# A graph layer on one core: 8 of 17 quads of edges grouped instead of 4 of 9, and their work moved in the order

## The chip, the cores and the metric

The kernel runs on one core of one Trainium2 chip. The metric is the time of one execution on the device in microseconds (us); less is better. A core has TensorE (PE, matrix products, with its weight loads listed apart as PEld), VectorE (DVE), ScalarE (ACT), GpSimd (POOL) and SyncE (SP, which here only issues transfers). TensorE writes to PSUM, which the kernel cuts into eight tiles of 512 f32 columns a partition (tags A and B, four each).

## The reference

One layer of a graph network on 6250 nodes with 128 features and 200000 edges; a node's messages are summed over its edges.

```python
h = jnp.maximum(_layernorm(x, axis=-1), 0.0)
...
idx_i = pair_indices[0]      # src: random in 0..6249
idx_j = pair_indices[1]      # dst: sorted
x = atomic_embedding @ W_in
W_ij = shifted_softplus(f_ij @ W_f1 + b_f1) @ W_f2 + b_f2
W_ij = W_ij * f_ij_cutoff
x_ij = x[idx_j] * W_ij
out = jax.ops.segment_sum(x_ij, idx_i, num_segments=N_ATOMS)
return shifted_softplus(out @ W_o1 + b_o1) @ W_o2 + b_o2
```

The result is added to the layer's input. An edge has 20 features and one cutoff weight. Edges are sorted by dst, from which they read, and not by src, to which their messages are added.

## The kernel before

**Tiling.** 128 edges are a chunk, four chunks a quad; 1563 chunks make 391 quads, and the main loop (L1220 on) takes one a step, in software-pipelined stages: at step i TensorE multiplies the edge features of quad i + 1 (`s1_pe`, z, L326) and, for quad i - 1, reads its 128-row inputs from a window of the node table by a one-hot product (xg, L510) and makes the filter (W, L507 and L518); ScalarE takes exp and ln of z and scales xg by the cutoff (xc, L523); VectorE multiplies W by xc (`s2_m`, L533), which gives the 512 messages of the quad. Node features are prepared along the way in 25 groups (`prep_*`), edge features split into three bf16 parts in 49 blocks (`fb_*`, L276 to L299).

**Three ways for a message.** The list `mpq` names the quads that are *grouped*; before, four of every nine from quad 8 on, 168 in all. The other 223 go by GpSimd.

- *Plain* quads (31: the first 12 and the last 19 of those not grouped): VectorE compares all pairs of src in a chunk (`s1_eq`, eq, L370), TensorE adds up messages of the same src (pp, L545), ScalarE copies, and GpSimd adds each chunk to one of four accumulators in DRAM by an indirect transfer (`scatter`, L595). Edges that aren't the first of their src go to a row that nobody reads.
- *Listed* quads (192, in 12 windows of 16): duplicates are found ahead of time, in pairs of quads (`l_eq`, L382, `l_count`, L391); messages are scattered straight from the tile s, and a window's duplicates go to rows of their own, which are summed and scattered later (`l_*`).
- *Grouped* quads use no scatter for most edges. Nodes are cut into 16 groups of 392. For eight quads at a time VectorE ranks edges within their group (`rank_*`, L601 to L669) and gives each of them one of 32 slots of its group or one of 64 overflow slots. `perm_oh` (L675) makes the one-hot of slots, `part_rem` (L689) splits the messages (tile pt, two buffers) into high and remaining bf16 parts, `permute` (pq, L700) puts them in slots by sixteen products of 387 columns, and `perm_out` (L706) copies each of four slices. After eight quads, a *round*, four *unit* calls (`unit_oh` L779, `unit_pe` un, L794, `unit_evac` L805) add the slots to the nodes of four groups each, in SBUF (accT), by 96 products on 32 rows each. Steps with a unit call are those of `unit_its`; `clear` moves other TensorE work out of their way.
- *Overflow* of a grouped quad (64 slots): `over_pe` (po, L715 to L717) gathers it by twelve products on 64 columns, in the lower or upper half of a tile that two grouped quads share; these also add up the three parts; `over_out` (L723) copies the sum into mo. For each such pair duplicates are summed by a product (`over_row`, `over_eq`, `over_sum`) and 128 rows are scattered.

**Order.** It is written out by hand: `at(step, point, function)` files work under a step and a point of it, and the loop runs the points in a fixed order; each engine takes its own instructions in that order. What matters here: "L" (loads, SP's queue), then on VectorE "D0", oh, "D1", eq, "DM", the message product, index work, "D2"; on TensorE xg and W of i - 1, z of i + 1, pp of i - 2, then "PE2"; on ScalarE the activations, "A0", "A1", xc, then what "PE2" and "A2" bring. Within a point, hooks run in the order in which they were filed. A buffer that is taken again waits for its last reader, wherever that stands in the order of another engine.

**Start and end.** Before the loop the accumulators' zeros begin to be written (GpSimd's and SP's queues, until about step 23). `RET` retires the first accumulator for the last 64 scatters, and it is added to accT by 13 transposes (`r0_*`) while the loop ends. After the last scatter the other three are loaded, summed, transposed and added (tp, L1388), and two products with the activation between them and the layer's input make the result.

## Time and profile before

Three runs took 2062.51, 2064.37 and 2069.87 us, median 2064.37. The profiled execution took 2051.26 us.

| | us | share of the span |
|---|---|---|
| profiled execution, whole | 2051.26 | |
| its span, first to last instruction | 2049.5 | 100% |
| TensorE busy | 1855.4 | 91% |
| VectorE busy | 1658.4 | 81% |
| GpSimd busy | 1636.9 | 80% |
| ScalarE busy | 1491.2 | 73% |
| mean granted clock of TensorE | | 0.966 of full speed |

In the profile's rows a group stands as line, engine, operation, tile written <- tiles read, shape and count, then busy time and mean duration of one, then the idle time of the engine just before them and what ended it. Matmuls overlap, so their busy time is less than count times duration. Rows of waits read: engine and line, what it waited for, us in total, times, longest. Timelines give start, duration and count.

### The profile page before, as it was taken

To read this page: it belongs to the slowest core of one execution; us is meant where nothing else is said; L and a number is where in the kernel's file an instruction comes from. 1 tells how busy PE (TensorE), PEld (TensorE's weight loads), DVE (VectorE), ACT (ScalarE), POOL (GpSimd) and SP (SyncE) were. 2 spreads that over 40 slices of the span, in tenths; PEclk is the share of its full clock that TensorE was granted. 3 is DMA by queue.
4 is the path that set the end of the run, shared out by engine and by line. 5 is a ranking of instruction groups with operands and counts; after the bars stand their busy time and mean duration, and the time that the engine had idled before them with its cause. 6 is when DMAs were issued, how large, how long until landed. Compare 5 with 4: busy or idle time off the path is not lost. (4 is left out here: it accounts for less than half of the span.)

```text
span 2049.5 us, 57496 instructions
## 1 busy us (share of the span) xinstructions
PE 1855.4 (91%) x20381; PEld 1284.7 (63%) x20381; DVE 1658.4 (81%) x4449; ACT 1491.2 (73%) x4083; POOL 1636.9 (80%) x1040
## 2 busy tenths in 40 slices
PE   3579999999999999999999999999999999999966
PEld 2456666666666666666666666666666666677734
DVE  4578898798888888988888978879898887787745
ACT  3468776877777788777778777777877778788714
POOL 3578888888888888887878778888888888888884
PEclk9689999999999999999999999999999999999987
DMA  6887666667666676766667666676676666666747
GB/s 239 228 210 154 124 123 121 129 110 140 126 126 119 118 139 119 131 127 120 120 121 132 120 117 123 110 125 127 121 131 108 129 126 109 112 123 125 141 44 252
DMA packets 359686, 272.58 MB, mean 133 GB/s; under 512 B 97727, under 2 KB 319850, under 8 KB 359394
## 3 DMA queue, kind: packets, MB, share of 16 engines
q0 software_dynamic: 143728, 71.30, 34.9%
q1 hardware_dynamic: 215378, 197.50, 32.9%
q8 instruction: 161, 2.64, 0.5%
q14 instruction: 131, 1.07, 0.2%
q10 hardware_dynamic: 288, 0.07, 0.0%
HBM read 154.45 MB, written 114.24 MB: 131 GB/s over the span
## 5 line engine op out<-in xcount | busy, mean ns | idle before, releaser
L595 POOL DMA_INDIRECT acc<-s,lji x768 | 1242.7, 1618 | 254.5 <-issue 185.8
L700 PE MATMUL pq<-pt,pm 128*128 128x387 bf16 x2688 | 533.6, 342 | 33.6 <-DVE pt L689 10.5
L523 ACT ACTIVATE xc<-xg,cb 128x128 f32<-128x128 f32 x1564 | 447.7, 372 | 111.5 <-PE xg L510 101.8
L518 PE MATMUL W<-w,a 128*128 128x128 f32 x3128 | 465.3, 293 | 0.0
L518 PEld LDWEIGHTS W<-w,a 128*128 128x128 f32 x3128 | 389.6, 196 | 42.3 <-issue 3.1
L706 ACT CAST mst<-pq 128x387 bf16<-128x387 f32 x672 | 303.7, 482 | 135.0 <-PE pq L700 132.3
L700 PEld LDWEIGHTS <-pm 128*128 128x128 bf16 x2688 | 261.0, 99 | 221.5 <-issue 26.6
L794 PE MATMUL un<-so,mst 32*128 32x392 bf16 x8064 | 371.0, 326 | 12.9 <-DVE pr L640 6.4
L794 PEld LDWEIGHTS <-mst 32*128 32x128 bf16 x8064 | 223.9, 93 | 153.4 <-issue 51.0
L336 ACT ACTIVATE a<-a,con 128x512 f32<-128x512 f32 x391 | 282.3, 722 | 12.8
L331 ACT ACTIVATE a<-z 128x512 f32<-128x512 f32 x391 | 237.8, 608 | 32.9 <-PE z L326 18.0
L595 POOL DMA_INDIRECT acc<-s,ji x123 | 196.0, 1594 | 78.7 <-issue 26.5
L689 DVE TENSOR_TENSOR pt<-pt 128x512 f32<-128x512 f32 x336 | 231.7, 689 | 5.8
L675 DVE TENSOR_SCALAR pm<-iot,pos 128x576 bf16<-128x576 f16 x672 | 221.0, 390 | 0.0
L533 DVE TENSOR_TENSOR s<-W,xc 128x512 f32<-128x512 f32 x192 | 131.9, 687 | 89.1 <-ACT xc L523 84.9
L805 DVE TENSOR_TENSOR accT<-un,accT 128x392 f32<-128x392 f32 x320 | 158.5, 558 | 55.1 <-PE un L794 55.0
L779 DVE TENSOR_SCALAR so<-iot,mst 128x392 bf16<-128x392 f16 x672 | 192.6, 346 | 5.4 <-PE un L794 5.3
L595 POOL DMA_INDIRECT acc<-os,oji x96 | 156.9, 1635 | 30.7 <-issue 15.6
L510 PE MATMUL xg<-wn,oh 63*128 63x128 bf16 x1564 | 157.5, 222 | 14.8 <-ACT xc L523 8.2
L326 PE MATMUL z<-ft,ws 123*128 123x512 bf16 x391 | 151.9, 389 | 15.7 <-POOL b2rep L940 9.3
L507 PE MATMUL W<-b2rep,onesb 64*128 64x512 bf16 x391 | 154.1, 394 | 0.0
L533 DVE TENSOR_TENSOR pt<-W,xc 128x512 f32<-128x512 f32 x168 | 115.3, 686 | 44.1 <-ACT xc L523 36.0
(210 smaller groups left out, 2431.3 us busy)
## 6 DMA issues: line engine op xcount, KB each, us to landing
rb<-reld SPq DMA_DIRECT2D x391, 64.0 KB
fsd<-f SPq DMA_DIRECT2D x49, 480.0 KB
ft<-fsd SPq DMA_DIRECT2D x195, 120.0 KB
sb<-src SPq DMA_DIRECT2D x169, 128.0 KB
fb<-in_fB_dram SPq DMA_DIRECT2D x49, 320.0 KB
ft<-fsd SPq DMA_DIRECT2D x195, 80.0 KB
wn<-tab SPq DMA_DIRECT2D x782, 15.8 KB
acc<-s,lji POOLq DMA_INDIRECT x768
```

The lines of the kernel that those rows point to most:

```text
L331: nc.scalar.activation(a, st[q]["z"], AF.Exp)
L336: nc.scalar.activation(a, a, AF.Ln, bias=half, scale=0.5)
L518: nc.tensor.matmul(W[:, c, :], st[q]["a"][:, c * P:(c + 1) * P], w2, start=False, stop=(c == 3))
L523: nc.scalar.mul(xc[:, c, :], st[q]["xg"][:, c, :], late["c", q // CQ][:, 4 * (q % CQ) + c:4 * (q % CQ) + c + 1])
L533: nc.vector.tensor_tensor(m[:, :, :P], st[q]["W"], st[q]["xc"], op=ALU.mult)
L595: nc.gpsimd.indirect_dma_start(out=accs[k][:rows, :], out_offset=bass.IndirectOffsetOnAxis(ap=ji, axis=0), in_=s, in_offset=None, compute_ ...
L675: nc.vector.tensor_scalar(pm[:, c], iot[:, :SLOTS], rk[r]["pos"][:, 4 * j + c:4 * j + c + 1], None, op0=ALU.is_equal)
L689: nc.vector.tensor_tensor(pt[:, :, k * P:(k + 1) * P], a, high(a), op=ALU.subtract)
L700: nc.tensor.matmul(t[:, :PW], mp[q]["pm"][:, c, s * P:(s + 1) * P], high(mp[q]["pt"][:, c:c + 1, :PW])[:, 0], start=(c == 0), stop=(c == 3))
L706: nc.scalar.copy(mp[q]["ms", s][:, :PW], mp[q].pop(("q", s))[:, :PW])
L779: nc.vector.tensor_scalar(so, iotw[:, :GN], w[:, 3 * P // 2:3 * P // 2 + 1], None, op0=ALU.is_equal)
L794: nc.tensor.matmul(ts[g][:, :GN], mp[q]["ms", s][v, k * P:(k + 1) * P], mp[q]["oh"][v], start=(q == qs[0] and k == 0), stop=(q == qs[-1] a ...
```

## The change

The list of grouped quads starts at 2 and takes 8 of 17, which makes 184 of 391; 176 quads are listed, in 11 windows, and 31 are plain. A round still has eight quads and four unit calls, now at four evenly spaced steps of the 17. Two new points are run right before pp: "DR", where `part_rem` now stands, and "PE1", where `over_pe` and `over_out` now stand, for both quads of a pair at once, in the step in which the next pair's first message is multiplied. `over_pe` issues four products for each quad, alternately for the lower and the upper 64 columns, on all three parts at 387 columns; mo holds the parts in bf16, and `over_sum` makes three bf16 products in place of one f32. Rank steps lie at fixed distances before their first quad. Splits of edge features (`fb_*`) and loads and comparisons of listed quads are moved to unit steps, and the maximum of a block (`fb_max`) to three steps earlier. The two halves of the second index load lie in unused columns of accT. The fourth accumulator's zeros are issued by step 20. The scratch for GpSimd's descriptors is set to 8192 bytes, where it stood at the default.

```diff
@@ -25,13 +25,13 @@
...
 SLOTS = GRP * CAP + OVC
-MP0 = 8
-MPGAPS = (2, 2, 2, 3)
+MP0 = 2
+MPGAPS = (2, 2, 2, 2, 2, 2, 2, 3)
 MPEND = 0
...
 RKQ = 8
-UOFF = (2, 6)
+UOFF = (2, 6, 10, 14)
 SW = 16
...
@@ -77,7 +77,7 @@
...
     K1_END, K2_END, K3_END = 2, 8, 140
-    Z2, Z3 = [0,0,1,1,2,2,3,3,4,4], [5+2*j for j in range(10)]
+    Z2, Z3 = [0,0,1,1,2,2,3,3,4,4], [5, 7, 9, 11, 13, 14, 16, 17, 19, 20]
     mpq = sorted_quads(NQ)
...
@@ -150,7 +150,7 @@
...
     for i in range(2):
-        mo_ = cp.tile([P, 132], F32, name=f"mo{i}")
+        mo_ = cp.tile([P, PW + 1], BF16, name=f"mo{i}")
         mos.append(mo_)
...
@@ -169,8 +169,8 @@
...
         v = accs[k][ACC_R:].rearrange("(p t) f -> p (t f)", p=P)
-        w = LR // ZL
-        nc.sync.dma_start(v[:, j * w:(j + 1) * w], zero[:, :w])
+        a, b = j * LR // ZL, (j + 1) * LR // ZL
+        nc.sync.dma_start(v[:, a:b], zero[:, :b - a])
 
...
@@ -283,8 +283,10 @@
...
 
+    def fb_max(b):
+        nc.vector.tensor_reduce(fmax[:, b:b + 1], fst[b]["f"], axis=AX.X, op=ALU.max, apply_absolute_value=True)
+
     def fb_2(b):
-        nc.vector.tensor_reduce(fmax[:, b:b + 1], fst[b]["f"], axis=AX.X, op=ALU.max, apply_absolute_value=True)
         fr = wk.tile([P, FE], F32, tag="fr", name="fr", bufs=1)
...
@@ -706,29 +708,25 @@
...
     def over_pe(q):
-        h = mpi[q] % 2 * OVC
+        qs = mpq[mpi[q] // 2 * 2:mpi[q] + 1]
         t = ps.tile([P, 512], F32, tag="B", name="po", bufs=4)
-        o = t[h:h + OVC]
         for c in range(4):
-            w = mp[q]["pm"][:, c, GRP * CAP:]
-            pt = high(mp[q]["pt"][:, c:c + 1])[:, 0]
-            nc.tensor.matmul(o[:, :P + 3], w, pt[:, 2 * P:PW], start=(c == 0), stop=False)
-            nc.tensor.matmul(o[:, :P], w, pt[:, P:2 * P], start=False, stop=False)
-            nc.tensor.matmul(o[:, :P], w, pt[:, :P], start=False, stop=(c == 3))
-        mp[q]["po"] = t
+            for h, p in enumerate(qs):
+                nc.tensor.matmul(t[h * OVC:(h + 1) * OVC, :PW], mp[p]["pm"][:, c, GRP * CAP:],
+                                 high(mp[p]["pt"][:, c:c + 1, :PW])[:, 0], start=(c == 0), stop=(c == 3))
+        mp[q]["po"] = t, len(qs) * OVC
 
     def over_out(q):
-        h = mpi[q] % 2 * OVC
+        t, n = mp[q].pop("po")
         mo = mos[mpi[q] // 2 % 2]
-        nc.scalar.copy(mo[h:h + OVC, :P + 3], mp[q].pop("po")[h:h + OVC, :P + 3])
-
-    def over_none(q):
-        nc.vector.memset(mos[mpi[q] // 2 % 2][OVC:, :P + 3], 0.0)
+        nc.scalar.copy(mo[:n, :PW], t[:n, :PW])
+        if n < P:
+            nc.vector.memset(mo[n:, :PW], 0.0)
 
...
         so = sp_.tile([P, 1], F32, tag="ovs", name="ovs", bufs=3)
-        nc.vector.scalar_tensor_tensor(so, mo[:, P + 2:P + 3], float(GN), mo[:, P + 1:P + 2], op0=ALU.mult, op1=ALU.add)
+        nc.vector.scalar_tensor_tensor(so, mo[:, PW - 1:PW], float(GN), mo[:, PW - 2:PW - 1], op0=ALU.mult, op1=ALU.add)
         mp[q]["so"] = so
...
@@ -745,13 +743,16 @@
...
     def over_eq(q):
-        eq = wk.tile([P, P], F32, tag="oeq", name="oeq", bufs=1)
+        eq = wk.tile([P, P], BF16, tag="oeq", name="oeq", bufs=1)
         nc.vector.tensor_scalar(eq, mp[q].pop("row")[:, :P], mp[q]["so"], None, op0=ALU.is_equal)
...
         t = ps.tile([P, 512], F32, tag="B", name="osum", bufs=4)
-        nc.tensor.matmul(t[:, :P + 4], mp[q]["eq"], mos[mpi[q] // 2 % 2][:, :P + 4], start=True, stop=True)
+        mo = mos[mpi[q] // 2 % 2]
+        nc.tensor.matmul(t[:, :P + 4], mp[q]["eq"], mo[:, 2 * P:], start=True, stop=False)
+        nc.tensor.matmul(t[:, :P], mp[q]["eq"], mo[:, P:2 * P], start=False, stop=False)
+        nc.tensor.matmul(t[:, :P], mp[q]["eq"], mo[:, :P], start=False, stop=True)
         mp[q]["sum"] = t
...
@@ -920,6 +921,7 @@
...
         prep_tp(0)
+        fb_max(0)
         fb_2(0)
...
@@ -948,7 +950,7 @@
...
         for mo_ in mos:
-            nc.vector.tensor_copy(mo_[:, P + 3:P + 4], wgt)
+            nc.vector.tensor_copy(mo_[:, PW:PW + 1], wgt)
         idl = cp.tile([P, max(NW, 1)], F32, name="idl")
...
@@ -977,7 +979,8 @@
...
         def half_load(k):
-            t_ = wk.tile([HALF, 2, SEG], I32, tag="pm", name="half")
+            o = NP - 2 * (2 - k) * SEG
+            t_ = accT[:HALF, o:o + 2 * SEG].bitcast(I32).rearrange("p (a e) -> p a e", a=2)
             v = slice(k * SEG, (k + 1) * SEG)
...
@@ -1016,9 +1019,13 @@
...
         for b in range(1, NB):
-            t0 = 2 if b == 1 else 8 * b - 8
+            t0 = 2
             if b > 1:
-                at(max(0, t0 - 3), "L", fb_load, b)
+                t0 = 8 * b - 8
+                while (t0 - MP0 + 1) % sum(MPGAPS) not in UOFF:
+                    t0 -= 1
+                at(max(0, t0 - 6), "L", fb_load, b)
+            at(max(t0 - 3, 1), "D2", fb_max, b)
             at(t0, "A1", fb_1, b)
...
@@ -1125,11 +1132,11 @@
...
             i = mpq[RKQ * r]
-            at(i - 5, "D2", rank_group, r)
-            k = clear(i - 4, units)
-            at(k, "PE2", rank_count, r)
-            at(k + 1, "D0", rank_own, r)
-            k = clear(k + 1, units)
+            i = max(i, 6)
+            at(i - 6, "D2", rank_group, r)
+            at(i - 5, "PE2", rank_count, r)
+            at(i - 4, "D0", rank_own, r)
+            k = mpq[RKQ * r] if i == 6 else i - 2
             at(k, "PE2", rank_over, r)
...
@@ -1139,6 +1146,8 @@
...
                 i = splain[n] + 2 if w else 6 + 2 * g
+                while w and (i - MP0) % sum(MPGAPS) not in UOFF:
+                    i -= 1
                 for k in range(2):
...
@@ -1174,25 +1183,22 @@
...
             at(q + 1, "D2", perm_oh, q)
-            at(q + 2, "D2", part_rem, q, 1)
-            at(q + 2, "D2", part_rem, q, 2)
+            at(q + 2, "DR", part_rem, q, 1)
+            at(q + 2, "DR", part_rem, q, 2)
             at(q + 2, "A2", part_ext, q)
...
                     at(q + 3, "PE2", perm_out, q, s)
-                at(q + 3, "PE2", over_pe, q)
-                at(q + 3, "PE2", over_out, q)
             else:
...
                     at(q + 4 + s // 2, "A0", perm_out, q, s)
-                at(q + 4, "PE2", over_pe, q)
-                at(q + 5, "A0", over_out, q)
-            if q == mpq[-1] and mpi[q] % 2 == 0:
-                at(q + 4, "D2", over_none, q)
             if mpi[q] % 2 or q == mpq[-1]:
+                k = mpq[mpi[q] + 1] + 1 if mpi[q] + 1 < len(mpq) else q + 3
+                at(k, "PE1", over_pe, q)
+                at(k, "PE1", over_out, q)
                 at(q + 5, "DM", over_idx, q)
...
@@ -1207,7 +1213,7 @@
...
             for s, k in enumerate(unit_slots(mpq, r)):
-                at(k - 2, "D2", unit_oh, r, s, 0)
+                at(k - (1 if (k - MP0) % sum(MPGAPS) != UOFF[0] and k < last else 2), "D2", unit_oh, r, s, 0)
                 at(k - 1, "D2", unit_oh, r, s, 1)
...
@@ -1249,6 +1255,8 @@
...
                 s3_idx(i - 3)
+            run(i, "DR")
+            run(i, "PE1")
             full[i] = sum(fn in banked for fn, _ in hooks.get((i, "PE2"), [])) > 2
...
@@ -1513,7 +1521,7 @@
...
 def prep_start(g):
-    busy = unit_its(sorted_quads(4 * PREP_GAP * (g + 8)))
+    busy = unit_its(sorted_quads(4 * PREP_GAP * (g + 10)))
     return clear(7 + PREP_GAP * (g - 1), busy, 2) - 1
...
@@ -1603,7 +1611,7 @@
...
     n_nodes, n_edges = inputs["x"].shape[0], inputs["src"].shape[0]
-    nc = bacc.Bacc("TRN2", target_bir_lowering=False, num_devices=1)
+    nc = bacc.Bacc("TRN2", target_bir_lowering=False, num_devices=1, dynamic_dma_scratch_size=8192)
     arrays, args = {}, []
...
         a = np.ascontiguousarray(a)
```

## What was predicted

> **What bounds the kernel now.** I read the profile's page first, then the busy time of each engine in three stretches, cut at the first-layer product (L326) of quad 18 and at that of the last quad, 390.
>
> ```profile
> span 2049.5 us, 57496 instructions
> ...
> PE 31%; DVE 6%; DMA 3%; ACT 3%; POOL 2%; issue 2%; SPq 1%; DVEq 0%; POOLq 0%; ACTq 0%
> ```
> ```profile
> core 0: us, PE busy (x) PEld busy (x) DVE busy (x) ACT busy (x) POOL busy (x), PEclk, DMA share, GB/s
> 0.00:147.50 147.50, 78.78 (x501) 58.35 (x501) 82.31 (x217) 65.05 (x176) 78.57 (x71) 0.80 0.79 226
> 147.50:1945.60 1798.10, 1712.44 (x19244) 1181.80 (x19242) 1524.68 (x4120) 1391.92 (x3840) 1492.24 (x922) 0.99 0.68 125
> 1945.60:2049.50 103.90, 64.20 (x641) 44.51 (x640) 51.42 (x114) 34.23 (x70) 66.08 (x48) 0.83 0.60 148
> ```
>
> In the long middle TensorE is busy 1712 of 1798 us and leads the chain; 86 us are idle. VectorE has 1525 us (85%). GpSimd's 1492 us look like slack, but its scatters stand back to back, at the end of the loop as elsewhere:
>
> ```profile
> 1991.27 1.54 POOL L595 DMA_INDIRECT acc<-s,ji  x1 [0.30 <-issue]
> 1993.12 1.54 POOL L595 DMA_INDIRECT acc<-s,ji  x1 [0.30 <-issue]
> 1994.96 1.54 POOL L595 DMA_INDIRECT acc<-os,oji  x1 [0.30 <-issue]
> ```
> ```profile
> L595 POOL DMA_INDIRECT acc<-s,lji x768 | 1242.7, 1618 | 254.5 <-issue 185.8 <-DMA acc<-s,lji 20.4 <-DVE s L533 18.5
> ...
> L533 DVE TENSOR_TENSOR s<-W,xc 128x512 f32<-128x512 f32 x192 | 131.9, 687 | 89.1 <-ACT xc L523 84.9 <-DMA acc<-s,lji 2.5 <-PE pq L700 0.6
> ```
>
> One scatter takes 1.85 us from start to start, of which 0.30 us is issue that isn't counted as busy. So GpSimd is nearly full too. But it is not the pace: VectorE, which refills the buffers that scatters empty, waited for a landed scatter only 2.5 us in the whole run. TensorE is the pace in the middle, GpSimd is late at the end.
>
> **The change, part by part.** *TensorE, work added.* 184 quads are grouped instead of 168 (the list is cut to rounds of eight). Between the two cuts ten more quads are permuted (175 against 165, by the iterations that the hooks name) and seven more unit calls fall (87 against 80): four of the old kernel's 84 calls and five of the new one's 92 come after the last cut.
>
> ```profile
> L700 PE MATMUL pq<-pt,pm 128*128 128x387 bf16 x2640 | 521.1, 340 | 32.6 <-DVE pt L689 9.6 <-DVE rt L664 8.2 <-ACT pt L695 5.3
> ...
> L794 PE MATMUL un<-so,mst 32*128 32x392 bf16 x7680 | 349.0, 324 | 9.0 <-DVE pr L640 6.4 <-DVE loh L422 1.3 <-ACT os L759 0.9
> ```
>
> These are the middle's own rows: 521.1/165 = 3.16 us a quad and 349.0/80 = 4.36 us a call, so +31.6 and +30.5 us.
>
> *TensorE, overflow.* Before, each quad has twelve matmuls on 64 columns:
>
> ```profile
> 144.74 0.69 PE L700 MATMUL pq<-pt,pm 128*128 128x387 bf16 x3
> 145.35 0.25 PE L715 MATMUL po<-pt,pm 128*64 128x131 bf16 x1
> 145.44 0.22 PE L716 MATMUL po<-pt,pm 128*64 128x128 bf16 x1
> ...
> 146.03 0.22 PE L717 MATMUL po<-pt,pm 128*64 128x128 bf16 x1
> 146.18 0.39 PE L507 MATMUL W<-b2rep,onesb 64*128 64x512 bf16 x1
> ```
> ```profile
> 1858.41 1.40 PE pq L700 x8
> ...
> 1861.22 0.22 PE z L326
> ```
>
> From 145.35 to 146.18 it is 0.83 us, and 0.08 us more go where the three permuting matmuls (175 ns each, by the eight in 1.40 us) turn to 64 columns: 0.91 us, 165 times = 150 us. After, a pair of quads has eight matmuls of 387 columns, alternately on the lower and the upper 64 columns. No such neighbours stand in the trace. The bounds: both halves run together, 4 x 0.175 = 0.70 us, or one after the other, 1.40 us; 0.17 us for the two turns on top. Over the 87 pairs between the cuts that is 76 or 137 us, so -74 or -13 us. I take -74: the nearest row is that of the units, where four matmuls on different 32 rows last 324 ns each and yet 7680 fill 349 us, 45 ns each, so they run four at a time.
>
> The Trainium skill (TensorE: Matmul & The Clock Gate, Part 3, "What overlaps and what doesn't") says that weights load beside a running matmul only when the row groups differ, which two halves of the columns don't. By it the loads of a pair would stand bare; what that would cost is the second rival. This trace disagrees for one tile, in the row below. The same page's table of goals has small-M matmuls on different column groups running together (2.38 times for three); no run here shows it yet.
>
> ```profile
> L716 PEld LDWEIGHTS <-pm 128*64 128x64 bf16 x672 | 73.0, 109 | 10.7 <-issue 10.3
> ```
>
> Twelve such loads of 109 ns would be 1.3 us bare, and the twelve matmuls with their loads took 0.83 us.
>
> *Small TensorE work.* One window of sixteen listed quads goes (11 for 12), and the overflow's sum takes three bf16 matmuls (60 ns apart, as L716's) for two f32 passes:
>
> ```profile
> L754 PE MATMUL osum<-mo,oeq 128*128 128x132 f32 x168 | 35.5, 293 | 0.0
> ...
> L391 PE MATMUL lcnt<-wgtb,eql 128*128 128x1 bf16 x768 | 26.0, 163 | 0.9 <-DVE accT L805 0.7 <-DVE accT L803 0.2
> ...
> L482 PE MATMUL lsum<-lm,leq 128*128 128x128 f32 x96 | 15.9, 293 | 7.6 <-DMA lm<-acc 3.7 <-DVE leq L476 3.6
> ```
>
> (26.0 + 15.9)/12 = 3.5 us, and 84 x (35.5/84 - 0.18) = 20 us of modelled busy time, of which I count 4, as two f32 passes follow each other in half their modelled length. Middle: 31.6 + 30.5 - 74 - 3.5 - 4 = **-19 us** (with the halves one after the other +42).
>
> *TensorE, idle.* Three waits go or shrink. Remainders come before the other late VectorE work, and the ranks are counted one iteration earlier and never meet a unit:
>
> ```profile
> PE pq L700 <- DVE pt L689: 9.6, 16, 1.3
> PE pq L700 <- DVE rt L664: 8.2, 7, 1.7
> ...
> PE un L794 <- DVE pr L640: 6.4, 7, 1.4
> ```
>
> That is up to 24 us. What is late next is VectorE itself. Ten more grouped quads cost it permutation one-hots, remainders, unit one-hots and evacuations, and lose half a listed comparison:
>
> ```profile
> L689 DVE TENSOR_TENSOR pt<-pt 128x512 f32<-128x512 f32 x336 | 231.7, 689 | 5.8
> L675 DVE TENSOR_SCALAR pm<-iot,pos 128x576 bf16<-128x576 f16 x672 | 221.0, 390 | 0.0
> ...
> L779 DVE TENSOR_SCALAR so<-iot,mst 128x392 bf16<-128x392 f16 x672 | 192.6, 346 | 5.4 <-PE un L794 5.3
> L805 DVE TENSOR_TENSOR accT<-un,accT 128x392 f32<-128x392 f32 x320 | 158.5, 558 | 55.1 <-PE un L794 55.0
> ...
> L382 DVE TENSOR_TENSOR eql<-sb,srcT_sb 128x1024 bf16<-128x1024 int16 x96 | 116.7, 1216 | 25.6 <-DMA sb<-src 23.1 <-PE W L518 2.2 <-issue 0.3
> L533 DVE TENSOR_TENSOR pt<-W,xc 128x512 f32<-128x512 f32 x168 | 115.3, 686 | 44.1 <-ACT xc L523 36.0 <-PE z L326 4.2 <-PE W L518 2.8
> ```
>
> (231.7 + 221.0 + 192.6 + 158.5)/168 - 116.7/192 = 4.2 us, x 10 = 42 us, to 1567 us. There is also a **new wait**. The message tile pt has two buffers, and a pair's overflow now reads both of them in the iteration in which the next pair's first message is to be written. That write (L533) so waits behind the overflow on TensorE: 0.22 us for z, 0.87 us for the overflow. Queued behind it on VectorE are the index of a plain quad, the remainders and everything late. Bounds: 0, and 92 x 1.1 = 101 us. VectorE was idle 44.1 us before 168 such writes, 0.26 us each, and a writer that comes late anyway loses nothing, so I take a third, 34 us, and let half of it reach TensorE: +17. Idle: -24 + 17 = **-7 us**.
>
> *Moved.* Feature splits and the listed comparisons go to iterations with a unit call, and the blocks' maxima three iterations earlier.
>
> ```profile
> L289 DVE TENSOR_TENSOR fr<-fb,f 128x640 f32<-128x640 f32 x49 | 40.2, 821 | 2.1 <-ACT f L283 2.1
> ```
>
> Nothing is added, and while TensorE runs a call of 4.36 us, a subtraction of 0.82 us or a comparison of 1.22 us keeps nobody waiting; without that cover both stand ahead of a message, as they may now. On SP's queue a block's load is issued three iterations earlier; its write still holds up the loads behind it until VectorE's second subtraction, which gains or loses nothing that I can name. ScalarE copies a pair's overflow once, 387 columns wide, instead of twice 131: at nothing, in the time that TensorE's next permutations take.
>
> *Ramp.* Of the first 18 quads eight are grouped instead of five, so three fetch no broadcast indices and issue no scatters.
>
> ```profile
> q0 software_dynamic: 143728, 71.30, 34.9%
> ...
> sb<-src SPq DMA_DIRECT2D x169, 128.0 KB
> ```
>
> Each saves 128 KB and four scatters of 71.30 MB/987 = 72 KB (987 with the lists' and overflows' own), together 1.25 MB; at the ramp's 226 GB/s and a DMA share of 0.79 this is 5.5 us. Their extra TensorE and VectorE work fits in the ramp's idle halves (78.78 and 82.31 of 147.5 us). Zero pieces and index halves are issued earlier on SP's queue, which I count at nothing: **-6 us**, bounds -15 and +10.
>
> *End.* What follows the last z now:
>
> ```profile
> 1945.64 0.38 PE L326 MATMUL z<-ft,ws 123*128 123x512 bf16 x1
> ...
> 1978.97 5.82 PE L794 MATMUL un<-so,mst 32*128 32x392 bf16 x93 [1.33 <-DVE accT L1091]
> ...
> 2007.87 1.11 PE L1388 MATMUL tp<-idt,ta_in 128*128 128x128 f32 x4 [21.77 <-DMA ta_in<-acc]
> ```
>
> TensorE idles 21.8 us for GpSimd's late scatters, the last issued 49.3 us after z. After, 56 scatters fewer (931) leave no backlog: the last 19 plain quads spread over 35 iterations instead of 29. But five unit calls follow z instead of four, for the last grouped quad is 390 itself. TensorE then has three permutations (9.5 us), the unit of iteration 390 (4.4), two overflows and two quads (some 4.5), 3 us of latency and four calls at some 6 us: 45 us. The last overflow's scatter goes out after the second of the four, about 35 us after z, and its loads land 13 us on (as 1994.96 to 2007.87), at 48. With the 41.6 us from 2007.87 to the end this makes 90 for 104 us: **-14 us**.
>
> Sum: -19 - 7 - 6 - 14 = -46 us. The profiled execution took 2051.3 us, 1.8 of them around its span, and becomes 2005. It lies 13.1 us under the median of the runs, 2064.4, so the runs should give **2018 us** (2.2% less).
>
> The scratch for GpSimd's descriptors is also set, to 8192 bytes. Nothing in the trace shows that room; a landing is shown once in the chain:
>
> ```profile
> 1607.31 5.40 DMA acc<-s,lji
> ```
>
> At 5.4 us to land and one every 1.85 us three scatters are in flight. Room for three costs nothing, which I take; room for one would make each 5.4 us.
>
> **Rivals.** *The halves run one after the other.* For: no column halves are seen together. Against: the row tiles are. +61 us: **2079 us**, slower by 0.7%; it decides as soon as a pair's overflow takes 1.4 us.
>
> *Their weights load bare as well.* 8 x (0.175 + 0.109) + 0.17 = 2.4 us a pair, 212 us for 76: **2154 us**. Against: the 0.83 us above, in which twelve loads were hidden.
>
> *VectorE becomes the bound* through the new wait. For: 85% busy in the middle now, 1567 of some 1770 us after, 89%. Against: it is often late, and then the wait is covered. If every pair pays its 1.1 us, two thirds of the 101 us reach TensorE, 67 in place of 17: **2068 us**, the gain gone. It decides from about half of that on.
>
> *GpSimd is the pace after all.* For: 1.85 us without a pause. Against: the 2.5 us above. 56 x 1.85 = 104 us: **1960 us**, which TensorE's idle time, 86 us and 22 at the end, just allows.
>
> **How the numbers follow.** Forecast 0.56; the halves one after the other 0.12; bare weights 0.02; VectorE 0.18; GpSimd 0.10; the set scratch costs something, 0.02. From 1975 to 2085 us holds the forecast, the first rival and VectorE's, and leaves out 0.14; the likeliest case alone spans 1985 to 2045, which is the ramp's bounds and the idle time's with the wait at nothing or at twice what I take. A difference of 0.5%, 10 us, is about what measurements of this kernel can tell from none. VectorE's case lies about zero, 0.02 faster, 0.10 same and 0.06 slower. Faster: 0.56 + 0.10 + 0.02 = 0.68. Same: 0.10 and 0.02 of the first rival's, 0.12. Slower: 0.10 + 0.02 + 0.06 + 0.02 = 0.20.
>
> **What would show it.** An overflow of a pair in 0.8 or 1.6 us; the L533 write of pt with a wait for po; TensorE's idle time in the middle near 79 us; waits on L689, L664 and L640 gone; the wait before the first tp under 10 us; scatters still 1.85 us apart but with pauses. The forecast is wrong if TensorE's busy time in the middle rises, or its idle time doesn't fall.

## The result: slower, and where the time went

The kernel after takes 2143.5 us (median of four runs, 2139.7 to 2144.0) beside 2066.5 us for the kernel before in the same session: a ratio of 1.0375 (95% interval 1.0353 to 1.0397), 3.75% slower, where 2.2% faster was predicted. Below, a difference between two kernels in us is the difference of their ratios to the kernel before, times 2066.5 us.

The busy times of the kernel after in three stretches, cut at z of quad 18 and of quad 390 as before (columns: length, then busy time and count for TensorE, its weight loads, VectorE, ScalarE and GpSimd, then the granted clock, the DMA share and GB/s):

```profile
span 2137.9 us, 57194 instructions
```
```profile
0.00:142.50 142.50, 79.08 (x524) 54.23 (x525) 91.15 (x243) 68.86 (x186) 64.85 (x62) 0.88 0.78 229
142.50:2040.40 1897.90, 1750.58 (x18879) 1123.86 (x18879) 1562.88 (x4274) 1408.11 (x3847) 1453.72 (x887) 0.97 0.63 116
2040.40:2137.90 97.50, 72.27 (x782) 47.95 (x781) 59.45 (x142) 40.52 (x84) 48.76 (x36) 0.92 0.53 144
```

The ramp is 5.0 us shorter and the end 6.4 us shorter. All of the loss, 99.8 us between these two profiles, is in the middle. There TensorE is busy 38 us longer (1750.6 against 1712.4) and idle 62 us longer (147.3 against 85.7). The profiled execution of the kernel before was a quick one, 15 us under its median, so the profiles differ by 88 us where the runs differ by 77. Experiment 1 below is the same kernel with a setting that costs nothing, and its middle is longer:

```profile
145.70:1964.90 1819.20, 1713.73 (x19245) 1182.30 (x19243) 1525.02 (x4120) 1383.06 (x3839) 1503.26 (x925) 0.99 0.68 123
```

Beside it the middle grows by 79 us, TensorE's busy time by 37 and its idle time by 42. So the idle time that the change adds is 42 to 62 us.

VectorE's 1562.9 us are those that were forecast (1567). GpSimd, which was taken for 1492.2 us and 922 issues of 0.305 us, 1774 of 1798 us, now has 174 us to spare. Its waits:

```profile
POOL acc L597 <- issue: 210.5, 690, 0.3
POOL acc L597 <- DVE s L535: 148.6, 48, 8.7
POOL acc L597 <- ACT ji L578: 61.1, 17, 16.1
```

So the scatters do pause, as foretold, and it is worth nothing, for they now wait for VectorE's messages.

The next table is worked out from the trace. In the middle, every TensorE instruction is charged the time to the start of the next one; idle time in it is in brackets, and stands with the instruction ahead of it (what z's row holds is the wait of what comes after z):

```
charged to    before, us          after, us
pq            524.6 (idle 22.2)   573.8 (33.4)
un            352.6 ( 9.0)        385.7 (10.1)
po            137.2 ( 0.0)         74.8 ( 1.2)
osum           29.9 ( 6.4)         22.1 ( 3.3)
z             123.5 (28.1)        171.1 (61.5)
orow           29.4 ( 4.6)         48.9 (18.1)
rkp            10.9 ( 0.0)         22.1 ( 9.8)
all others    590.0 (15.4)        599.4 ( 9.9)
sum          1798.1 (85.7)       1897.9 (147.3)
```

Without the idle time, permutations are up 38.0 us, unit calls 32.0, overflow down 63.6 and its sum 4.7: the four items that the prediction costed come to +2, where it gave them -16. The other 98 us are idle time (62) and 36 us on lines whose work hardly changed; 6 of these are plain quads' pp products, 168 for 128, because the last plain quads now spread over a longer stretch.

Another cause runs through these figures, the clock. The traces list the stretches in which TensorE was granted half of its clock: in the middle of the kernel after 26 of them, 113 us, in that of the kernel before 9, 44 us (8 and 37.5 us in experiment 1). In one of them the eight products of W, 1.16 us long in the iteration ahead, take 2.08 us (the second view has the granted clock, 0.50, in the third column from the end):

```profile
1147.65 1.16 PE L520 MATMUL W<-w,a 128*128 128x128 f32 x8
...
1156.80 2.08 PE L520 MATMUL W<-w,a 128*128 128x128 f32 x8
```
```profile
1156.20:1158.70 2.50, 2.50 (x15) 2.18 (x15) 0.00 (x0) 1.63 (x5) 2.19 (x2) 0.50 0.58 61
```

TensorE was busy for 104.6 us of these stretches, in the kernel before for 38.7 (30.3 in experiment 1). If work takes twice as long in them, half of that is lost: 33 us more than before (37 beside experiment 1), nearly all that TensorE's busy time grew by. Of the 33, 12 lie on permutations, 8 on unit calls, 5 on W. Counted at full clock the four items come to -19 us, close to the -16 of the prediction, and the 36 us on other lines are 25. A matmul's end in the profile is modelled, so what of these 25 isn't pp may be lateness that is counted as busy; this is not shown. The slow stretches follow stalls: in the 3.4 us ahead of each of the 26, which is the length of the shortest, TensorE was idle for 44% or more, 62% on the mean, and over the whole middle for 8%.

The overflow of a pair, on the timeline (start, duration, engine, line):

```profile
1008.95 0.38 PE L328 MATMUL z<-ft,ws 123*128 123x512 bf16 x1
1009.26 0.89 PE L715 MATMUL po<-pt,pm 128*64 128x387 bf16 x8
1010.08 2.97 PE L702 MATMUL pq<-pt,pm 128*128 128x387 bf16 x16
```

Eight matmuls of 387 columns take 0.82 us: the halves of the columns run together, and their weights load under them. What TensorE, VectorE and ScalarE waited for (us in total, times, the longest):

```profile
PE pq L702 <- ACT mst L708: 18.0, 8, 2.7
PE un L795 <- DVE so L780: 17.9, 12, 2.0
...
PE tp L1396 <- DMA ta_in<-acc: 10.6, 1, 10.6
PE pq L702 <- DVE pr L642: 9.2, 3, 3.7
PE pq L702 <- DVE rt L666: 8.7, 8, 1.9
```
```profile
DVE pt L535 <- PE po L715: 77.3, 38, 4.9
DVE s L535 <- ACT xc L525: 51.9, 51, 4.4
DVE pt L535 <- ACT xc L525: 29.1, 19, 2.7
```
```profile
ACT oji L769 <- DVE ojd L765: 90.3, 52, 5.3
```

and ScalarE of the kernel before:

```profile
ACT oji L768 <- DVE ojd L764: 40.2, 34, 2.5
```

The remainders' wait is gone, the ranks' waits are as large as before, and no single wait of TensorE is long enough to explain 62 us. Two things stand out on the engines that feed it: VectorE's new wait on pt, 77.3 us, and ScalarE's wait for the overflow's scatter index, which went from 40.2 to 90.3 us. The second is not a change that the diff makes anywhere. One iteration of the kernel after shows how it comes about (the one ahead of a round's first quad; in brackets the idle time of the engine before it, and what ended it):

```profile
1148.65 0.38 PE L328 MATMUL z<-ft,ws 123*128 123x512 bf16 x1
...
1149.45 0.81 DVE L287 TENSOR_REDUCE fmax<-fb 128x1 f32<-128x640 f32 x1
1150.18 1.20 DVE L677 TENSOR_SCALAR pm<-iot,pos 128x576 bf16<-128x576 f16 x4
1151.29 0.19 DVE L660 SCALAR_TENSOR_TENSOR ra<-cnt,rank 128x32 f32<-128x32 f32 x1
...
1152.26 0.19 DVE L666 SCALAR_TENSOR_TENSOR rt<-rko,ov 128x32 f32<-128x32 f32 x1
...
1152.50 0.94 PE L702 MATMUL pq<-pt,pm 128*128 128x387 bf16 x4 [1.87 <-DVE rt L666]
...
1152.68 0.22 DVE L765 SCALAR_TENSOR_TENSOR ojd<-os,con,ojd 128x1 f32<-128x1 f32 x1
1152.81 0.69 DVE L535 TENSOR_TENSOR s<-W,xc 128x512 f32<-128x512 f32 x1
1152.93 0.29 ACT L769 ACTIVATE oji<-ojd,con 128x1 int32<-128x1 f32 x1 [3.05 <-DVE ojd L765]
...
1153.22 0.59 ACT L333 ACTIVATE a<-z 128x512 f32<-128x512 f32 x1
...
1153.77 1.80 POOL L597 DMA_INDIRECT acc<-s,lji  x1 [4.55 <-DVE s L535]
...
1154.46 0.36 ACT L237 ACTIVATE h<-hps 128x256 f32<-128x256 f32 x1
...
1154.88 1.45 PE L702 MATMUL pq<-pt,pm 128*128 128x387 bf16 x4 [1.44 <-ACT h L237]
```

VectorE is behind: the block's maximum, four one-hots and the ranks' slots stand ahead of the index ojd. ScalarE, which works in order, stands 3.05 us at oji for it, and behind oji queue the activation of a z that has been ready for 4.2 us and h, for which TensorE then waits another 1.44 us. TensorE waits in both lines for one of the four PSUM tiles of tag B; rt is the last reader of one, h of the other. After them, from 1153.1 on, the granted clock is a half for 6.8 us. From this z to the next it is 10.0 us, where the middle's mean is 5.1 (1897.9/372).

### The profile page after: what moved, and what is told of

Same layout as the page of the kernel before. It is cut to its first block, busy times and chain, and to the rows that moved or that the text cites. A ratio compares the mean times of both kernels' runs of the same rounds, so it can differ in the third digit from the quotient of the medians.

```text
span 2137.9 us, 57194 instructions
## 1 busy us (share of the span) xinstructions
PE 1901.9 (89%) x20181; PEld 1226.0 (57%) x20181; DVE 1713.5 (80%) x4656; ACT 1517.5 (71%) x4116; POOL 1567.3 (73%) x984
## 5 line engine op out<-in xcount | busy, mean ns | idle before, releaser
L597 POOL DMA_INDIRECT acc<-s,lji x704 | 1151.1, 1635 | 352.9 <-issue 165.3
L702 PE MATMUL pq<-pt,pm 128*128 128x387 bf16 x2944 | 589.4, 345 | 59.8 <-ACT mst L708 18.0
L702 PEld LDWEIGHTS <-pm 128*128 128x128 bf16 x2944 | 286.4, 100 | 280.4 <-issue 98.8
L795 PE MATMUL un<-so,mst 32*128 32x392 bf16 x8832 | 405.2, 329 | 30.6 <-DVE so L780 17.9
L708 ACT CAST mst<-pq 128x387 bf16<-128x387 f32 x736 | 336.3, 482 | 133.7 <-PE pq L702 103.5
L795 PEld LDWEIGHTS <-mst 32*128 32x128 bf16 x8832 | 241.5, 94 | 187.9 <-issue 45.0
L691 DVE TENSOR_TENSOR pt<-pt 128x512 f32<-128x512 f32 x368 | 253.5, 689 | 6.4
L535 DVE TENSOR_TENSOR pt<-W,xc 128x512 f32<-128x512 f32 x184 | 126.6, 688 | 147.4 <-PE po L715 77.3
L677 DVE TENSOR_SCALAR pm<-iot,pos 128x576 bf16<-128x576 f16 x736 | 239.9, 387 | 0.0
L597 POOL DMA_INDIRECT acc<-os,oji x103 | 172.4, 1674 | 49.8 <-issue 17.7
L806 DVE TENSOR_TENSOR accT<-un,accT 128x392 f32<-128x392 f32 x352 | 174.2, 557 | 24.7 <-PE un L795 19.0
L535 DVE TENSOR_TENSOR s<-W,xc 128x512 f32<-128x512 f32 x176 | 121.0, 687 | 81.6 <-ACT xc L525 51.9
```

The source lines that it names most:

```text
L535: nc.vector.tensor_tensor(m[:, :, :P], st[q]["W"], st[q]["xc"], op=ALU.mult)
L597: nc.gpsimd.indirect_dma_start(out=accs[k][:rows, :], out_offset=bass.IndirectOffsetOnAxis(ap=ji, axis=0), in_=s, in_offset=None, compute_ ...
L677: nc.vector.tensor_scalar(pm[:, c], iot[:, :SLOTS], rk[r]["pos"][:, 4 * j + c:4 * j + c + 1], None, op0=ALU.is_equal)
L691: nc.vector.tensor_tensor(pt[:, :, k * P:(k + 1) * P], a, high(a), op=ALU.subtract)
L702: nc.tensor.matmul(t[:, :PW], mp[q]["pm"][:, c, s * P:(s + 1) * P], high(mp[q]["pt"][:, c:c + 1, :PW])[:, 0], start=(c == 0), stop=(c == 3))
L708: nc.scalar.copy(mp[q]["ms", s][:, :PW], mp[q].pop(("q", s))[:, :PW])
```

## The experiments

**Experiment 1** sets only the scratch.

```diff
-    nc = bacc.Bacc("TRN2", target_bir_lowering=False, num_devices=1)
+    nc = bacc.Bacc("TRN2", target_bir_lowering=False, num_devices=1, dynamic_dma_scratch_size=8192)
```

> The kernel before with only the descriptor scratch set to 8192 bytes. If the smaller scratch throttles the scatters, they spread from 1.85 us apart and a good part of the loss shows here alone, 2090 to 2140 us. By the three other theories (new wait on pt, more grouped quads, order of the late work) the scratch is harmless: within 0.5% of 2066.5, that is 2056 to 2077 us, scatters still 1.85 us apart.

Measured: 0.9992 of before (0.9974 to 1.0010). The scratch costs nothing.

**Experiment 2** has the old grouping with every other edit.

```diff
-MP0 = 2
-MPGAPS = (2, 2, 2, 2, 2, 2, 2, 3)
-UOFF = (2, 6, 10, 14)
+MP0 = 8
+MPGAPS = (2, 2, 2, 3)
+UOFF = (2, 6)
```

> The kernel after, but with the old grouping (4 of 9 from quad 8, units at offsets 2 and 6 of 9); every other edit stays, the paired overflow with its wait on pt too. If the new wait is the loss, it is nearly all still here (84 pairs for 92): 2115 to 2140 us. If the grouping is the loss (eight rounds of the same step pattern in 17, 16 quads more), this stands below the kernel before, for it keeps the paired overflow: 2010 to 2060 us. If the order of ranks, remainders and lists is the loss: 2100 us or more.

Measured: 0.9994 (0.9975 to 1.0012), 2065.6 us. The new wait on pt is in it (59.6 us of VectorE's idle time), yet the loss is gone, so the wait alone is not the loss and the grouping is needed for it. But the paired overflow's saving doesn't show either. Its middle:

```profile
147.50:1958.80 1811.30, 1682.14 (x17995) 1089.13 (x17995) 1513.80 (x4115) 1374.31 (x3756) 1511.33 (x924) 0.97 0.67 123
```

TensorE is busy 30 us less than before (1682.1) and idle 43 us more (32 and 24 beside experiment 1). GpSimd has 1511.3 us and 924 issues of 0.305 us, 1793 of 1811 us: it is taken to 99%.

**Experiment 3** moves the pair's overflow to the end of TensorE's work of the iteration before.

```diff
-                at(k, "PE1", over_pe, q)
-                at(k, "PE1", over_out, q)
+                at(k - 1, "PE3", over_pe, q)
+                at(k, "A0", over_out, q)
...
             run(i, "A2")
+            run(i, "PE3")
```

> The kernel after, with the pair's overflow matmuls at the end of TensorE's work of the iteration before the one in which the next pair's first message is written, and ScalarE's copy of it at the start of that iteration. The write of pt then finds its buffer free. If the new wait is the loss: the 77 us of idle time that VectorE has ahead of L535 for po go and the time falls by 50 to 80 us, to 2065 to 2095 us. If grouping or the order of the late work is the loss, VectorE idles elsewhere and the time falls by 20 us at most: 2120 to 2145 us.

Measured: 1.0545 (1.0505 to 1.0585), 35 us slower than after. Neither theory had this. The wait of L535 for po is gone, and TensorE now waits in order for what the overflow reads and for a PSUM buffer, while VectorE waits the more for ScalarE:

```profile
PE po L715 <- DVE pt L691: 29.7, 16, 19.3
PE po L715 <- ACT mst L708: 20.5, 24, 2.1
```
```profile
DVE pt L535 <- ACT xc L525: 134.1, 57, 4.8
```

It says nothing on the price of the wait itself, since it made others; experiment 12 does.

**Experiment 4** puts remainders, ranks, feature splits and lists back.

```diff
-            at(q + 2, "DR", part_rem, q, 1)
+            at(q + 2, "D2", part_rem, q, 1)
...
-                while w and (i - MP0) % sum(MPGAPS) not in UOFF:
-                    i -= 1
...
+                at(i - 5, "D2", rank_group, r)
+                k = clear(i - 4, units)
+                at(k, "PE2", rank_count, r)
```

> The kernel after, with three placements as before: remainders with the late VectorE work, ranks five and four iterations ahead and clear of units, feature splits and listed comparisons not moved to unit iterations. If the pile of work in the iteration five ahead of a round's first quad is the loss (60 us of TensorE's idle and slowed time lie in that iteration of 17), this falls by 30 to 60 us, to 2085 to 2115 us. If the new wait or the grouping is the loss: 2135 to 2165 us, the three placements being worth what I counted for them in the prediction, up to 24 us of waits on remainders and ranks that come back.

Measured: 1.0337 (1.0297 to 1.0376), 8 us below after, which is inside the intervals. The pile went, and another came, since the paired overflow stands earlier than the late work that now holds the remainders:

```profile
PE po L715 <- DVE pt L691: 62.6, 34, 10.4
```

This is worked out from the traces: TensorE's time beyond the usual distance of the same two neighbours (the 20th percentile), summed by the iteration's place in the period of 17, from iteration 19 to 385. Place 12 is five ahead of a round's first quad; units stand at 2, 6, 10 and 14.

```
place in 17                    11     12     13     14     16    all 17
after                        12.2   59.9    6.8    9.4   25.7   224.7 us
all three back (4)           12.0    7.8   49.5   22.5   10.0   230.8
ranks back (5)               14.3   19.1    9.1   31.7   28.4   205.3
ranks in the unit's (16)     51.1   21.8    2.5    9.2   25.6   216.8
index one later (17)         12.5   44.1    4.1    9.7   18.4   190.6
```

**Experiment 5** puts the ranks alone back.

```diff
-            at(i - 6, "D2", rank_group, r)
-            at(i - 5, "PE2", rank_count, r)
+            at(i - 5, "D2", rank_group, r)
+            k = clear(i - 4, units)
+            at(k, "PE2", rank_count, r)
```

> The kernel after, with only the ranks placed as before (from the second round on: grouped five iterations ahead, counted four ahead and clear of units). Theory A, the pile of work in the iteration five ahead of a round's first quad is a loss of its own: the 60 us of TensorE's idle and slowed time in that iteration of 17 fall to some 20, and the time to 2095 to 2115 us. Theory B, engines that wait for one another in turn, so that time saved at one wait comes up at the next: 2130 to 2150 us, with the same total of TensorE's idle and slowed time, about 225 us, at other iterations.

Measured: 1.0236 (1.0214 to 1.0259), 29 us below after by the ratios; in the two profiles the middle differs by 17 us. Between the theories: the place of the ranks is a loss, some 17 to 29 us of it. In the table above, 41 us leave place 12 and 22 come up at place 14, a unit's, where TensorE now waits for the ranks. ScalarE's wait for the scatter index falls too, from 90.3 us:

```profile
PE un L795 <- DVE pr L642: 16.6, 14, 2.0
```
```profile
ACT oji L769 <- DVE ojd L765: 57.2, 36, 5.3
```

**Experiment 6** has the old overflow under the new grouping: over_pe, over_out, over_sum and their buffers as before, at the old places.

```diff
-                at(k, "PE1", over_pe, q)
-                at(k, "PE1", over_out, q)
+                at(q + 4, "PE2", over_pe, q)
+                at(q + 5, "A0", over_out, q)
```

> The kernel after, with the overflow of each grouped quad by itself as before (twelve matmuls of 131 and 128 columns behind its permutations, sum in f32); grouping and order stay. TensorE gets 74 to 80 us of work back, the wait of L535 for po goes. If the pair's overflow is worth on the clock what it saves on TensorE less a small wait: 2190 to 2215 us. If it gives back by its wait all that it saves: 2130 to 2155 us. If the wait is the loss: under 2120 us.

Measured: 1.0754 (1.0731 to 1.0777), 78 us above after. That is just what was forecast for TensorE, 74 and 4 us, and the exact match is chance: between the middles of the two profiles 65 us of it are TensorE's busy time and 14 its idle time. All that is wrong lies in the rest: grouping and order cost 156 us together.

**Experiments 7 and 8** take scatters out of experiment 2's kernel and of the kernel before.

```diff
-            for c in range(nchunks(q)):
+            for c in range(nchunks(q) - 1):
```

> The second experiment's kernel (old grouping, every other edit) with the last of each listed quad's four scatters left out: 192 scatters less, 1.9 us each. It leaves part of the messages out of the sums. If GpSimd was the pace with the old grouping, and held back what the pair's overflow saves on TensorE, the time falls by 50 us or more, to 2015 us or less. If TensorE and VectorE waiting for each other are the pace: 2050 to 2065 us, little more than the end's late scatters (some 20 us).

> The kernel before with the same scatters left out, so part of the messages is missing from the sums. If GpSimd was its pace too: 2010 us or less. If TensorE was (1712 us busy of 1798 in the middle): 2035 to 2060 us, the end's wait for late scatters alone. The difference to the run beside it is what the paired overflow and the new order are worth where GpSimd is out of the way: 75 us by TensorE's work, near nothing if waits take it back.

Measured: 0.9819 (0.9786 to 0.9853) and 0.9952 (0.9939 to 0.9965). Relief of GpSimd is worth 36 us to experiment 2's kernel, less than the 50 that I had named, and 10 to the kernel before. With GpSimd out of the way, the change without its grouping is 28 us faster, and the grouping costs 115 us (1.0375 against 0.9819), or 105 if leaving out the same scatters would give the kernel after the 10 us that it gave the kernel before, which was not tried. The middle of experiment 7:

```profile
148.50:1920.40 1771.90, 1669.71 (x17996) 1082.76 (x17996) 1506.56 (x4117) 1375.90 (x3756) 1194.35 (x730) 0.98 0.62 118
```

From here to the kernel after the middle grows by 126 us. TensorE's permutations and unit calls, idle time left out, are 62 of these (29.0 and 33.1, charged as above), its idle time 45 (102.2 to 147.3). At full clock the 62 are 51; the half clock, 105 us of TensorE's busy time against 69, adds 18.

**Experiment 9** has old grouping and old overflow: the order alone, with the ramp's loads.

```diff
-UOFF = (2, 6, 10, 14)
+UOFF = (2, 6)
...
-                at(k, "PE1", over_pe, q)
+                at(q + 4, "PE2", over_pe, q)
```

> The kernel after with old grouping and old overflow: what is left of the change is the order of ranks, remainders, feature splits and lists (and the ramp's loads). Theory A, that order costs TensorE time by itself: the runs so far give 2224 - 2070 = 154 us for grouping and order together, of which grouping, by the rounds' own TensorE work of 62 us and its stalls, is about 110, so 2100 to 2125 us here. Theory B, the order is harmless (as I forecast: waits on remainders and ranks go) and the second experiment stood at 2066 only since GpSimd was full: 2040 to 2070 us, and grouping alone costs the 154 us.

Measured: 1.0154 (1.0126 to 1.0183), 32 us slower than before: between the theories, nearer to A. The new order costs time by itself.

**Experiment 10** is experiment 2's kernel with ranks, feature splits and lists as before; **experiment 11** is the same under the new grouping (the diff is that of experiment 4 without the remainders).

> The second experiment's kernel with ranks, feature splits and lists placed as before too: the kernel before with the paired overflow and the remainders ahead of the other late work (and the ramp's loads). Theory A: 25 us or more below the second experiment, 2010 to 2040 us, GpSimd's 987 scatters a little over 1.85 us apart being the floor. Theory B: 2055 to 2070 us as there.

> The kernel after with ranks, feature splits and lists placed as before, remainders left ahead of the other late work: the grouping's own price beside the run before. If the three placements add up (ranks 23 us by the fifth experiment) and the feature splits and lists are worth nothing: 2115 to 2125 us. If they too pile up in front of something: 2090 to 2110. If they help: 2130 or more, and the fourth experiment's loss was less than the remainders' place alone.

Measured: 0.9993 (0.9974 to 1.0012), so B's figure, and 1.0280 (1.0230 to 1.0330). The first has GpSimd at its limit like experiment 2, and what the order costs can't show there. The second, beside 1.0236 with the ranks alone put back, gives the feature splits and lists 9 us of gain if anything, and beside 1.0337 of experiment 4 the remainders' new place 12 us; in both cases the intervals overlap, so neither is shown.

**Experiment 12** gives pt a third buffer and moves nothing; **experiment 13** does so in experiment 11's kernel.

```diff
-        mp.setdefault(q, {})["pt"] = wk.tile([P, 4, PW], F32, tag="pt", name="pt")
+        mp.setdefault(q, {})["pt"] = wk.tile([P, 4, PW], F32, tag="pt", name="pt", bufs=3)
```

> The kernel after with a third buffer for the message tile pt, so that the next pair's first message finds a free one; nothing else moves. If the new wait is worth on the clock what VectorE idles for it (77 us): 2065 to 2080 us. If it is worth the 17 us that the prediction gave it: about 2125 us. If VectorE's idle time only comes up at the next write (for ScalarE's xc): 2135 to 2150 us.

> The eleventh experiment's kernel with the third buffer for pt. If the wait and the ranks' place are separate losses, the gain of the run before is found here again below the eleventh experiment (1.028 of before). If one covers the other, less. Were grouping, its TensorE work apart, free of stalls, this would stand at 2050 us; the 45 us that grouping cost beside its work in the runs so far say 2080 or more.

Measured: 1.0394 (1.0367 to 1.0421) and 1.0257 (1.0231 to 1.0283), both the same as without the third buffer (1.0375 and 1.0280). In experiment 12 VectorE's wait on po falls from 77.3 to 4.8 us, and its idle time stands, 91 us more at these two rows than in the kernel after (172.0 for 81.0), with the next operand of the same multiplication:

```profile
DVE s L535 <- ACT xc L525: 89.1, 86, 4.8
DVE pt L535 <- ACT xc L525: 82.9, 64, 3.4
```

The new wait was there, was as long as feared, and cost nothing: VectorE waited for po in place of waiting for xc.

**Experiment 14** is experiment 10's kernel with the scatters of experiments 7 and 8 taken out.

> The tenth experiment's kernel without the last scatter of each listed quad, so part of the messages is missing from the sums. If GpSimd (99% taken in the middle) is all that hides the paired overflow's 75 us there: 0.955 to 0.97 of before, against 0.995 of the kernel before with the same scatters out. If TensorE and VectorE hold each other up there as well: 0.98 to 0.99, as in the seventh experiment.

Measured: 0.9815 (0.9798 to 0.9833), as experiment 7. The middles of experiment 8 and of this:

```profile
147.00:1948.90 1801.90, 1711.50 (x19244) 1184.00 (x19243) 1514.94 (x4122) 1388.39 (x3840) 1187.14 (x731) 0.99 0.61 117
```
```profile
145.50:1909.40 1763.90, 1659.49 (x18011) 1083.16 (x18009) 1509.67 (x4122) 1371.99 (x3760) 1193.37 (x730) 0.99 0.63 119
```

TensorE is busy 52 us less and idle 14 us more: even with GpSimd out of the way, a quarter of what TensorE is relieved of comes back as waiting.

**Experiment 15** groups 172 quads in the old pattern, with ranks, feature splits and lists as before.

```diff
-MPGAPS = (2, 2, 2, 2, 2, 2, 2, 3)
-MPEND = 0
+MPGAPS = (2, 2, 2, 3)
+MPEND = 3
...
-EXTRA = 0
+EXTRA = 4
...
-LEARLY = 8
-LLATE = 16
+LEARLY = 16
+LLATE = 24
```

> 172 quads in the old pattern of 4 of 9, from quad 2 on, units at offsets 2 and 6 of 9, the last round with twelve quads; paired overflow, remainders ahead of the other late work, ranks, feature splits and lists placed as before; one listed window fewer. 15 scatters fewer (28 us of GpSimd), four quads more (17 us of TensorE), the units' calls the same 84. If GpSimd is the floor under the old grouping: 2025 to 2045 us, below both kernels. If not: 2055 to 2075 us.

Measured: 0.9951 (0.9933 to 0.9970), 2050.7 us beside 2059.7: 10 us faster than the kernel before, between the two cases that I had named.

**Experiment 16** moves the ranks' first step into the unit's iteration.

```diff
-            at(i - 6, "D2", rank_group, r)
+            at(i - (7 if i > 6 else 6), "D2", rank_group, r)
```

> The kernel after with one step moved: from the second round on, VectorE's grouping of a round (2.4 us) goes one iteration earlier, from the iteration that also evacuates a unit's four tiles into the unit's own iteration. If the pile in that iteration is what makes TensorE wait in the next (60 us of idle and slowed time in the iteration five ahead of a round's first quad): that falls to 20 us or less and the time to 2095 to 2115 us. If any place gives the same waits: 2135 to 2150 us.

Measured: 1.0437 (1.0421 to 1.0452), 13 us worse than after. Place 12 fell to 22 us, nearly as the first case had it, and place 11 rose to 51 (the table at experiment 4): the pile moved with the step. None of the three places tried is free, and my picture of one bad iteration was too simple.

**Experiment 17** moves ScalarE's conversion of the scatter index (the lists' likewise) from the end of an iteration to the start of the next.

```diff
-                at(k + 1, "A2", over_int, q)
+                at(k + 2, "A0", over_int, q)
```

> The kernel after with ScalarE's conversion of the overflow's (and the lists') scatter index moved from the end of an iteration to the next one's start, behind VectorE's part of it. If ScalarE's 90 us of waiting there hold up its copies of the next iteration (xc, mst), and so VectorE and TensorE: 2095 to 2125 us. If ScalarE only waits there in place of waiting for TensorE: 2135 to 2150 us.

Measured: 1.0220 (1.0204 to 1.0235), 32 us below after. Its middle, and what ScalarE and VectorE waited for:

```profile
143.90:2002.30 1858.40, 1734.61 (x18879) 1112.99 (x18879) 1561.73 (x4273) 1410.67 (x3847) 1447.09 (x887) 0.98 0.66 118
```
```profile
ACT oji L769 <- DVE ojd L765: 28.8, 25, 3.8
```
```profile
DVE pt L535 <- PE po L715: 113.1, 59, 5.2
```

ScalarE's wait falls from 90.3 to 28.8 us; TensorE is idle 23.5 us less and busy 16 us less with the same work; 82 us of the middle are at half clock instead of 113, and 77.0 us of TensorE's busy time instead of 104.6, which makes 14 of the 16. VectorE waits longer for po, 113 us, in a kernel that is 32 us faster. The iteration shown above now looks like this:

```profile
1129.26 0.38 PE L328 MATMUL z<-ft,ws 123*128 123x512 bf16 x1
...
1130.44 0.64 ACT L333 ACTIVATE a<-z 128x512 f32<-128x512 f32 x1
...
1133.28 0.22 DVE L765 SCALAR_TENSOR_TENSOR ojd<-os,con,ojd 128x1 f32<-128x1 f32 x1
...
1133.53 0.29 ACT L769 ACTIVATE oji<-ojd,con 128x1 int32<-128x1 f32 x1 [1.43 <-DVE ojd L765]
...
1135.22 0.38 PE L328 MATMUL z<-ft,ws 123*128 123x512 bf16 x1
```

VectorE reaches ojd as late as before, 4.0 us after z, but ScalarE has activated z meanwhile, and the next z comes after 6.0 us, not 10.0. The clock stays at full speed here.

**Experiment 18** puts both moves on the kernel of experiment 15.

> The fifteenth experiment's kernel (0.995 of before) with the ranks' first step in the unit's iteration, counted two iterations later, and the index conversion one iteration later. GpSimd's 972 scatters at the 1.95 us apart that they take when it never pauses, from 52 us on and with 62 us behind the last, end at 2010 us; so 0.975 to 0.99 of before if TensorE's waits for ranks (22 us there) and ScalarE's for the index go, 0.995 to 1.0 if GpSimd or other waits take their place.

Measured: 0.9953 (0.9939 to 0.9966), no better than experiment 15. Its middle:

```profile
143.80:1937.90 1794.10, 1685.47 (x18055) 1102.62 (x18054) 1517.85 (x4122) 1382.16 (x3804) 1495.32 (x916) 0.97 0.70 124
```

GpSimd has 1495.3 us and 916 issues of 0.305 us, 1775 of 1794 us. It is full again, at 1.96 us a scatter on the mean, so GpSimd probably hides what the two moves give; this kernel was not tried with fewer scatters.

## Why the prediction was wrong, step by step

*TensorE, work added.* About right: 62.1 us were forecast, 70 measured between the cuts (38.0 and 32.0), 62 against experiment 7. At full clock it is 50 (25.8 and 23.9), so the close figure is in part luck: somewhat less work than forecast, and a slower clock that nobody had counted.

*Overflow.* Right in mechanism and nearly in size: 0.82 us a pair for 0.70 and 0.17, and -63.6 us of TensorE's time for -74, since the old overflow was charged 137 us and not the 150 of the forecast. On the clock it is 78 us where TensorE and VectorE set it. The first rival, halves one after the other, would have shown 1.6 us a pair. The second, bare weights, falls as well. The Trainium skill (TensorE: Matmul & The Clock Gate, Part 3, "What overlaps and what doesn't") lets weights load beside a running matmul only for another row group. This trace disagrees: all eight loads of a pair are on the same rows, and the eight matmuls with them take 0.82 us.

*TensorE, idle, -24 + 17 = -7.* This is the step that failed. It took the three waits for gained and let VectorE's 42 us of added work lie in its free 15%, with the wait on pt as the only place where VectorE can be late. Measured is +62 us (+42 beside experiment 1), and 33 us (37) more through a term that the forecast left out: after its stalls TensorE ran at half clock, 113 us of the middle instead of 44. VectorE's total came out as forecast, but its time doesn't lie where it is free: it falls into the iterations round a unit, VectorE gets there late, and ScalarE, which in the same iteration waits for VectorE's index, hands the lateness on to z's activation, xc and the permutations' copies, and so to TensorE. Of the time of the kernel after, 32 us are shown to pass through that one wait (experiment 17); the same move was not tried on the kernel before, whose wait there is 40.2 us, so not all of the 32 need be part of the loss. Another 17 to 29 us come from the ranks' new place (5). As the wait for the index falls in experiment 5 as well, the two may be in part the same. They were not tried together; if they added up, 1.008 of before would be left, and the new grouping would still not pay.

*The new wait on pt, +17.* Right in that it would be there (77.3 us of VectorE's idle time lie inside the bounds of 0 and 101), wrong in its price, which is nothing (12, 13).

*Ranks, remainders, lists.* The forecast took the ranks' earlier place for up to 15 us of gain (the waits on rt and pr). The wait on rt is still there (8.7 us), that on pr went from the unit calls (6.4) to the permutations (9.2), and the place costs time. Only the remainders did what was said: their wait went from 10.5 us to 1.6 (what that is worth on the clock is inside the intervals of 4 and 11). One moved step was not costed at all: half of a unit's one-hots, for three units of four, go from two iterations ahead of the call to one. The wait of un for so, 17.9 us, was not among the waits of the kernel before; no run tries this alone.

*VectorE becomes the bound*, the third rival, came nearest, but its place was wrong (the wait on pt) and its 2068 us too low, for it still counted the removed waits as gained.

*GpSimd.* I put it aside because VectorE had waited only 2.5 us for landed scatters. The sum of busy time and issue, 1774 of 1798 us, was the better sign: under the old grouping nothing that TensorE saves shows (2, 10, probably 18) until scatters are taken out (7, 14). For the sign of the change this didn't matter, as grouping relieves GpSimd; its relief of 104 us was just not worth what grouping costs.

*Ramp, end, scratch.* -5.0 for -6; -6.4 for -14, with the wait before tp at 10.6 us for the under 10 foretold; 0 for 0.

What grouping costs is so settled in size (105 to 115 us with GpSimd out of the way, some 51 of them TensorE's own work at full clock) and in part by its path. The rest of its stalls, beyond what passes through the index and the ranks, was not taken apart, and the remainders' place under the old grouping was not tried alone.

## What to carry to other kernels

Before an engine's saved time is counted, add up every other engine's busy time and its fixed time per issue in that stage: here GpSimd's 1774 of 1798 us said that TensorE's savings would not show, and a mean of 85% on VectorE said nothing of the iterations in which it was late. Where engines work in order through a common iteration, an instruction that takes another engine's result of the same iteration hands its lateness to everything queued behind it; taking it one iteration later was worth 32 us. A stall costs more than its idle time where TensorE's clock falls after it, here by an estimated 33 us, so look at the granted clock before a longer busy time is read as more work. The length of a wait in the profile is not its price: 77 us went with a third buffer and the time stayed, so take a wait away alone before believing in it.

## What the runs showed that I had not expected

Two matmuls on the two halves of the columns start 3 to 5 ns apart and the next two 171 to 194 ns later (medians of the starts in the trace of after, 92 pairs of quads); eight matmuls of 387 columns take 0.82 us where one after the other, at 175 ns each, they would take 1.40. And GpSimd, when it never pauses, takes 1.95 us a scatter on the mean of the middle, not the 1.85 seen most often: some scatters last longer, as the one of 1.80 us above beside the usual 1.54.
